# One inverse root for two norms in a row, and a norm's weight and bias applied where its rows are turned

## The chip, the cores and the metric

The kernel runs on one core of a Trainium2 chip. The metric is the time of the whole kernel on the device in microseconds (us), as the median of several runs. The core's engines are TensorE (PE; its weight loads are PEld), VectorE (DVE), ScalarE (ACT), GpSimd (POOL) and SyncE (SP, which here only issues transfers).

## What is computed

Input x has 4 sequences of 1024 rows with 128 columns. Two blocks follow each other:

```python
x = _layernorm(x + mamba(x))            # selective scan, 256 channels x 16 states
x = _layernorm(x + attention_and_moe(x))

# attention_and_moe(hidden_states), cut:
resid = hidden_states
x = layer_norm(hidden_states, ln1_w, ln1_b)
...                                     # causal attention, 16 heads of 8
hidden = resid + (ctx @ o_w + o_b)
resid = hidden
xt = layer_norm(hidden, ln2_w, ln2_b)
logits = xt @ router_w                  # 16 experts, top 2, limited capacity
...
h = gelu(xin @ fc1_w + fc1_b)           # xin: rows of xt, sorted to experts
...
return resid + moe_out
```

Each norm subtracts a row's mean and divides by the root of its variance plus 1e-5. The norm that ends the first block and ln1, which starts the second, act on the same rows one after the other, with nothing between them.

## The kernel before

**Stages.** A test at the start (lines 164 to 207) bounds the attention scores by the norms of the weights; with these inputs it holds and the first branch of line 1307 runs. There the work goes in halves of a sequence, 512 rows in 4 tiles of 128: 8 halves, named (sequence, half).

1. `front` makes the scan's inputs: projections, convolution, step sizes. They go through DRAM.
2. `scans`: for each half 2 groups of channels with 4 state groups, 8 steps in all. A step on DVE is a product `h = u * b` (`begin`, line 444), four scans (line 454), and a product with `c` (`gather`, line 460); ACT makes the decay `da` (line 448), and PE sums the states (line 464). The first sequence is scanned alone.
3. `after_scans` (line 376) follows each half: gate, the scan's own norm (its inverse root is `ssm_rs`), output projection, residual. Then `normalise_in_pieces` with tag `lnx` ends the first block, in place on the rows `r`, and `on_half` hands them to `inputs`.
4. `inputs` (line 574) is attention's start: the norm `ln1` of `x1` into `xh`, four transposes on PE, an ACT step `xnT` that applies ln1's weight and bias while it leaves PSUM (they are per partition after the turn), and the projections to keys, queries and values, the first two split into three bf16 parts that go through DRAM.
5. `stream` runs attention on PE and ACT: scores, exponent, weighted values.
6. `rest_of_half` (line 733): division by the sums, output projection, residual `hid`, the norm `ln2` into `x2`, its weight and bias as two products of 128x512 with rows broadcast to all partitions, the store (to DRAM, or for the last two halves straight into `xrow`), four transposes, a copy `x2T`, and the router's product.
7. `routing` sends rows to their experts' slots in DRAM by indirect transfers from GpSimd. `experts` runs 16 experts: load 512 rows, transpose them, copy to `xeT`, two matmuls with a Gelu between, and scatter back. A last loop adds, norms and stores.

**Norms.** `normalise_in_pieces` (line 146) does `bn_stats` and `bn_aggr` on DVE for each of 4 tiles, adds the constant to the variances (`_ve`, line 137), raises them to -0.5 on GpSimd in one instruction of 128x4 (`_rs`, line 139), and then, after a `yield USE`, subtracts the mean and multiplies, tile by tile, on DVE (line 156).

**Order.** Once the first sequence is scanned, PE and DVE run in the order in which the program writes their instructions (`tc.manual_schedule(engines=pinned)`); ACT, GpSimd and SyncE are ordered by the framework. The order comes from generators: `scan_row` yields between the parts of a scan step, and after each such part `piece()` (line 1319) advances the other streams. `before` holds `after_scans` with `inputs`, `after` holds `rest_of_half`, `aside` the routing, and `attend` is one step of attention:

```python
for at in (USE, None):
    for s in (before, after, aside, loads):
        advance(s, at)
    if at == USE:
        next(attend)
```

A part behind `yield USE` runs ahead of the piece's attention step, a part behind a plain `yield` after it. So `yield USE` and the plain `yield` that follows take one piece together, and a second `yield USE` takes another piece. Between two pieces lie two scans or one product of a scan step on DVE.

Of the kernel before, what the change touches and what calls it, by code (L numbers as in the profile page):

```python
# [10 lines left out]
F32 = mybir.dt.float32  # L11
BF16 = mybir.dt.bfloat16
I32 = mybir.dt.int32
AF = mybir.ActivationFunctionType
# [37 lines left out]
def mamba_then_moe_block_kernel(ctx: ExitStack, tc: tile.TileContext, a: dict, out: bass.AP):  # L52
# [11 lines left out]
    def load_columns(name, vec, n, pool=const):  # L64
        return load(name, [P, n], vec.rearrange("(n p) -> p n", p=P), pool)
# [80 lines left out]
    def normalise_in_pieces(pool, src, dst, n, tag):  # L146

        st = pool.tile([P, n, 6], F32, tag=tag + "_st", name=tag + "_st")
        mv = pool.tile([P, n, 2], F32, tag=tag + "_mv", name=tag + "_mv")
        for i in range(n):  # L150
            nc.vector.bn_stats(st[:, i, :], src[:, i, :])  # L151
            nc.vector.bn_aggr(mv[:, i, :], st[:, i, :])  # L152
        r = inv_std(pool, mv[:, :, 1], n, tag)
        yield USE
        for i in range(n):
            nc.vector.tensor_scalar(  # L156
                dst[:, i, :], src[:, i, :], mv[:, i, 0:1], r[:, i : i + 1], ALU.subtract, ALU.mult
            )
# [7 lines left out]
    ln1_w = load_columns("ln1_w", a["ln1_w"], 1)  # L166
    ln1_b = load_columns("ln1_b", a["ln1_b"], 1)
    head_rows = load("head_rows", [P, HG], a["c_head_rows"])
    with ExitStack() as ph:
# [139 lines left out]
    def scans(ph, x1_pool, on_scans, on_half, spare_bank=lambda: None):  # L309
# [66 lines left out]
        def after_scans(b, hf, y):  # L376
# [55 lines left out]
            for i in range(TPH):  # L432
                nc.vector.scalar_tensor_tensor(
                    r[:, i, :], pa[:, i * P : (i + 1) * P], rs[:, i : i + 1], r[:, i, :], ALU.mult, ALU.add
                )
            yield from normalise_in_pieces(s2, r, r, TPH, "lnx")
            yield from on_half(b, hf, r)

# [85 lines left out]
    def attention_weights(wts):  # L524


        wq = wts.tile([P, P], F32, tag="wq", name="wq")
        wk = wts.tile([P, P], F32, tag="wk", name="wk")
        for w, wp in ((wq, a["q_w_pad"]), (wk, a["k_w_pad"])):
            nc.sync.dma_start(  # L530
                w.rearrange("m (h d) -> m h d", d=HD),
                wp.rearrange("m g (h r) -> m (g h) r", r=P // HG)[:, :, 0:HD],
            )
        qb = wts.tile([P, 1], F32, tag="qb", name="qb")
        kb = wts.tile([P, 1], F32, tag="kb", name="kb")
# [24 lines left out]
        return wq, wk, qb, kb, wv, wo, wr, vb, ob, sel_b, ln2_w, ln2_b, identb, mask_k  # L560

    def attention(ph, weights):

        wq, wk, qb, kb, wv, wo, wr, vb, ob, sel_b, ln2_w, ln2_b, identb, mask_k = weights
        p1 = ph.enter_context(tc.tile_pool(name="fat1", bufs=1, side="right"))
# [5 lines left out]

        def inputs(b, hf, x1, made):

# [157 lines left out]
        def rest_of_half(e, avs, rows):  # L733
# [75 lines left out]
    def attention_with_maxima(ph):  # L809
# [25 lines left out]
        ob = load("ob", [P, D], a["o_b"].unsqueeze(0).partition_broadcast(P), wts)  # L835
        ln2_w = load("ln2_w", [P, D], a["ln2_w"].unsqueeze(0).partition_broadcast(P), wts)
        ln2_b = load("ln2_b", [P, D], a["ln2_b"].unsqueeze(0).partition_broadcast(P), wts)
        sel_a = load("sel_a", [P, NG, H], a["c_sel_a"], wts)
# [13 lines left out]
        for b in range(B):  # L852
# [119 lines left out]
            for qt in range(2):  # L972
# [28 lines left out]
                normalise(p2, hid, x2, 4, "ln2")  # L1001
                nc.gpsimd.tensor_tensor(x2, x2, ln2_w.unsqueeze(1).to_broadcast([P, 4, D]), ALU.mult)
                nc.gpsimd.tensor_tensor(x2, x2, ln2_b.unsqueeze(1).to_broadcast([P, 4, D]), ALU.add)
                rest = x1[:, t0 : t0 + 4, :]
# [4 lines left out]
                x2T = p2.tile([P, 512], F32, tag="x2T", name="x2T")  # L1009
                nc.scalar.copy(x2T, pt)  # L1010
                pl = bank("pl")
# [220 lines left out]
    def experts(ph, weights, behind, sent, all_sent):  # L1232
# [10 lines left out]
        for e in range(E):  # L1243
# [63 lines left out]
    with tc.If(mild > 0) as cmp:  # L1307

        with ExitStack() as late:
            with ExitStack() as ph:  # L1310
# [39 lines left out]

                def on_half(b, hf, x1):

                    yield from attention_inputs(b, hf, x1, made)
                    stacked, vps = made[b]
                    middle.append(Step(b=b, qt=hf, x1=x1, stacked=stacked, vps=vps))
# [50 lines left out]
    with cmp.Else():  # L1406
        scan_done.clear()
        with ExitStack() as ph:
            bank = work_banks(ph)
            drain = lambda pieces: deque(pieces, maxlen=0)  # L1410

            def store_half(b, hf, x1):
                to_tokens(rest_d, b * TPB + hf * TPH, x1)
                yield
# [86 lines left out]
```

## Time and profile before

| | us |
|---|---|
| median of 3 runs | 1365.01 |
| range of the runs | 1358.34 to 1372.29 |
| span of the profiled execution | 1372.2 |
| PE busy | 941.3 (69%) |
| DVE busy | 899.7 (66%) |
| ACT busy | 644.2 (47%) |
| POOL busy | 257.0 (19%) |

The rows of the norms and of what the change touches, from the groups of instructions (line, engine, operation, tiles and shapes, count; then total and mean in ns of one; then the idle time ahead of it and what ended it):

```profile
L156 DVE TENSOR_SCALAR xh<-x,ln_mv,ln_rs 128x128 f32<-128x128 f32 x32 | 8.9, 342 | 5.6 <-POOL ln_rs L139 5.6
L151 DVE BATCH_NORM_STATS2 ln_st<-x 128x6 f32<-128x128 f32 x32 | 8.6, 267 | 0.0
L152 DVE BATCH_NORM_AGGREGATE ln_mv<-ln_st 128x2 f32<-128x6 f32 x64 | 11.6, 182 | 2.1
L783 DVE TENSOR_TENSOR x<-x,ln_w 128x512 f32<-128x512 f32 x8 | 5.5, 692 | 0.3
L1255 DVE COPY xeT<-pt_xe 128x512 f32<-128x512 f32 x16 | 10.3, 682 | 0.0
```

The profile names `x1` and `r` as `x`, and the tags `ln1` and `ln2` both as `ln`: `ln_st<-x` belongs to ln1 and `ln_st<-hid` to ln2. How the profile's other views are read is said where they are shown.

### The profile page before, as it was taken

How to read it: one execution, taken by the hardware profiler on the slowest of the kernel's cores; microseconds unless marked ns; L12 is line 12 of the kernel's file. 1: busy time of each engine (PE TensorE's matmuls, PEld its weight loads, DVE VectorE, ACT ScalarE, POOL GpSimd, SP SyncE). 2: the span in 40 equal slices, each digit the busy share in tenths (PEclk: the TensorE clock that was granted, in tenths of full speed). 3: DMA queues.
4: the chain of work that ended last, by engine and by line, in shares of the span. 5: the costliest groups of instructions: out<-in, count | busy, mean ns of one | idle time of the engine just before them, and what ended most of it. 6: DMA issues, size and time to landing. Idle time of an engine off the chain costs nothing. (4 is left out here: it accounts for less than half of the span.)

```text
span 1372.2 us, 14838 instructions
## 1 busy us (share of the span) xinstructions
PE 941.3 (69%) x5100; PEld 431.3 (31%) x5100; DVE 899.7 (66%) x1407; ACT 644.2 (47%) x887; POOL 257.0 (19%) x232
## 2 busy tenths in 40 slices
PE   4687552477998985688886589688488343699920
PEld 2232210143333333233334224235132012466620
DVE  2299789888977987887998996883461025111136
ACT  1457663246855863466772287652147220133300
POOL 0021011111101012102001110100004712344421
PEclk9898875658987997789896589878579565799965
DMA  3963667363614533443452431320755102222142
GB/s 83 339 213 131 233 215 241 119 188 111 194 60 132 158 104 109 138 133 119 139 160 91 135 114 45 93 60 26 197 159 166 50 18 87 76 66 64 41 115 87
DMA packets 171157, 171.81 MB, mean 125 GB/s; under 512 B 33424, under 2 KB 125840, under 8 KB 170944
## 3 DMA queue, kind: packets, MB, share of 16 engines
q1 hardware_dynamic: 153664, 142.94, 34.9%
q10 hardware_dynamic: 13312, 19.40, 3.9%
q0 software_dynamic: 4096, 8.43, 1.9%
q8 instruction: 42, 0.69, 0.2%
q14 instruction: 43, 0.35, 0.1%
HBM read 111.27 MB, written 59.44 MB: 124 GB/s over the span
## 5 line engine op out<-in xcount | busy, mean ns | idle before, releaser
L690 ACT ACTIVATE pr<-pst 128x1024 f32<-128x1024 f32 (+3 forms) x384 | 293.1, 811 | 130.9 <-PE pst L686 71.1
L680 PE MATMUL pst<-qst,kst 72*128 72x512 bf16 (+3 forms) x768 | 204.1, 366 | 53.4 <-ACT pr L690 39.3
L448 ACT ACTIVATE da<-dt_sp,a_neg 128x512 f32<-128x512 f32 x256 | 178.2, 720 | 122.8 <-DVE h L454 112.4
L697 PE MATMUL av<-pr,vp 128*32 128x512 f32 (+3 forms) x1536 | 188.8, 562 | 7.3 <-issue 4.0
L444 DVE TENSOR_TENSOR h<-u_sp,bt 128x2048 f32<-128x2048 f32 x64 | 145.3, 2274 | 18.4 <-DMA u_sp<-u_d 18.4
L454 DVE TENSOR_TENSOR_SCAN h<-da,carry,h 128x512 f32<-128x512 f32 x128 | 155.9, 1266 | 1.7 <-ACT da L448 1.7
L454 DVE TENSOR_TENSOR_SCAN h<-da,h 128x512 f32<-128x512 f32 x128 | 148.6, 1207 | 6.6 <-ACT da L448 6.6
L460 DVE TENSOR_TENSOR h<-h,ct 128x2048 f32<-128x2048 f32 x64 | 146.2, 2285 | 1.2 <-POOL carry L457 0.3
L464 PE MATMUL py<-h,sel 128*32 128x512 f32 x512 | 90.5, 787 | 72.8 <-DVE h L460 54.7
L680 PEld LDWEIGHTS <-kst 72*128 72x128 bf16 x768 | 65.2, 105 | 205.6 <-issue 186.5
L457 POOL COPY carry<-h 128x4 f32<-128x4 f32 x32 | 43.7, 1365 | 288.5 <-DVE h L454 288.5
L1260 ACT ACTIVATE hT<-ph,b 128x512 f32<-128x512 f32 x64 | 44.0, 687 | 107.3 <-PE ph L1259 105.8
L114 POOL DMA_INDIRECT xin<-xrow,put x64 | 62.1, 971 | 102.8 <-DVE same_e L1138 30.3
L139 POOL TENSOR_TENSOR ln_rs<-ln_ve,neg_half 128x4 f32<-128x4 f32 x16 | 34.6, 2161 | 238.9 <-DVE ln_ve L137 238.9
L114 POOL DMA_INDIRECT eout<-eo,to x64 | 61.4, 960 | 83.2 <-DVE eo L1271 49.1
L686 PE MATMUL pst<-mask_k,identb 128*128 128x128 bf16 x512 | 76.0, 235 | 0.0
L259 PE MATMUL pt_x<-xT,w_tap 128*128 128x512 f32 x128 | 61.6, 639 | 19.1 <-DMA xT<-in_xT_dram 9.8
L1259 PE MATMUL ph<-xeT,w 128*128 128x512 f32 x128 | 61.1, 610 | 8.1 <-DVE xeT L1255 7.5
L1266 PEld LDWEIGHTS po_e<-w,hT 128*128 128x128 f32 x512 | 61.5, 192 | 13.5 <-issue 12.3
L1266 PE MATMUL po_e<-w,hT 128*128 128x128 f32 x512 | 63.2, 276 | 0.1
L686 PEld LDWEIGHTS <-identb 128*128 128x128 bf16 x512 | 51.9, 107 | 32.7 <-issue 11.2
L1103 DVE COPY tot<-ptot 128x64 f32<-128x64 f32 (+1 forms) x6 | 2.0, 333 | 85.7 <-PE ptot L1100 85.7
(218 smaller groups left out, 1126.9 us busy)
## 6 DMA issues: line engine op xcount, KB each, us to landing
dt_sp<-dt_d SPq DMA_DIRECT2D x64, 256.0 KB
u_sp<-u_d SPq DMA_DIRECT2D x64, 256.0 KB
kst<-k_parts SPq DMA_DIRECT2D x96, 144.0 KB
qst<-q_parts SPq DMA_DIRECT2D x64, 144.0 KB
bt<-bc_d SPq DMA_DIRECT2D x32, 256.0 KB
ct<-bc_d SPq DMA_DIRECT2D x32, 256.0 KB
w<-in_fc_w_dram SPq DMA_DIRECT2D x32, 256.0 KB
xin<-clear SPq DMA_DIRECT2D x8, 516.0 KB
```

What stands on the lines that cost most here:

```text
L114: ins = nc.gpsimd.indirect_dma_start(out=dst[:, :], out_offset=bass.IndirectOffsetOnAxis(ap=rows, axis=0), in_=src, in_offset=None).ins
L259: nc.tensor.matmul(pt[:, cols], lhsT=w_tap[:, k, c * P : (c + 1) * P], rhs=xT[:, cols.start + k : cols.stop + k], start=(k == 0), stop=(k ...
L444: nc.vector.tensor_tensor(s.h, s.u, four(s.bt), ALU.mult)
L448: nc.scalar.activation(s.da[jl], s.dt[:, jl, :], AF.Exp, scale=a_neg[:, j, s.g : s.g + 1])
L454: ins = nc.vector.tensor_tensor_scan(h, s.da[jl], h, from_, ALU.mult, ALU.add).ins
L460: nc.vector.tensor_tensor(s.h, s.h, four(s.ct), ALU.mult)
L464: nc.tensor.matmul(s.py[jl * NR : (jl + 1) * NR, :], lhsT=sel, rhs=s.h[:, jl, :], start=(s.g == 0), stop=(s.g == NG_S - 1),)
L680: nc.tensor.matmul(pst[:, jj, :w], lhsT=ks[ki // TPH][jp][:, jj, ki % TPH * P : (ki % TPH + 1) * P], rhs=qs[jp][:, jj, q0:], start=True, s ...
L686: nc.tensor.matmul(pst[:, jj, :P], lhsT=identb, rhs=mask_k, start=False, stop=True)
L690: nc.scalar.activation(pr[:, :, :w], pst[:, :, :w], AF.Exp, scale=QSCALE)
L697: nc.tensor.matmul(av[32 * j : 32 * j + 32, q0:], lhsT=e.vps[ki // TPH][:, ki % TPH, v0 : v0 + 32], rhs=pr[:, jj, :w], start=(ki == 0), st ...
L1266: nc.tensor.matmul(po[:, i, :], lhsT=hT[:, c, i * P : (i + 1) * P], rhs=w2[e][:, c, :], start=(c == 0), stop=(c == NFC - 1),)
```

## The change

It does two things.

The rows that `lnx` would give have mean 0 and variance v/(v+e), where v is the variance of `r` and e = 1e-5. So ln1's factor on `r` itself is 1/sqrt(v + e) times 1/sqrt(v/(v+e) + e), which is 1/sqrt(v(1+e) + e*e). Both factors now come from one set of statistics: two small additions on DVE make `ve[0]` and `ve[1]`, and one power on GpSimd of 128x8 gives both. `inputs` first makes `xh` straight from `r` with the second factor, and later, behind `xnT`, norms `r` in place with the first for the residual.

The weight and bias of ln2 are no longer multiplied into the rows. They are loaded as columns at the start, and applied where the turned rows leave PSUM: in `x2T` for the router (ACT, with scale and bias) and in `xeT` for the experts (DVE, a `tensor_scalar` with two per-partition operands in place of a copy). The stored rows and the expert slots hold the plain norm.

```diff
+        mv = statistics(pool, src, n, tag)
+        r = inv_std(pool, mv[:, :, 1], n, tag)
+        yield USE
+        apply_norm(src, dst, mv, r, n)
...
     ln1_b = load_columns("ln1_b", a["ln1_b"], 1)
+    ln2_w = load_columns("ln2_w", a["ln2_w"], 1)
+    ln2_b = load_columns("ln2_b", a["ln2_b"], 1)
...
-            yield from normalise_in_pieces(s2, r, r, TPH, "lnx")
-            yield from on_half(b, hf, r)
+            mv = statistics(s2, r, TPH, "lnx")
+            ve = s2.tile([P, 2, TPH], F32, tag="lnx_ve", name="lnx_ve")
+            nc.vector.tensor_scalar(ve[:, 0, :], mv[:, :, 1], LN_EPS, None, ALU.add)
+            nc.vector.tensor_scalar(ve[:, 1, :], mv[:, :, 1], 1.0 + LN_EPS, LN_EPS * LN_EPS, ALU.mult, ALU.add)
+            inv = s2.tile([P, 2, TPH], F32, tag="lnx_rs", name="lnx_rs")
+            nc.gpsimd.tensor_tensor(
+                inv.rearrange("p k i -> p (k i)"), ve.rearrange("p k i -> p (k i)"), neg_half[:, : 2 * TPH], ALU.pow
+            )
+            yield USE
+            yield from on_half(b, hf, r, lambda dst, k: apply_norm(r, dst, mv, inv[:, k, :], TPH))
...
-        ln2_w = load("ln2_w", [P, D], a["ln2_w"].unsqueeze(0).partition_broadcast(P), wts)
-        ln2_b = load("ln2_b", [P, D], a["ln2_b"].unsqueeze(0).partition_broadcast(P), wts)
...
             xh = p1.tile([P, 4, D], F32, tag="tok", name="xh")
-            yield from normalise_in_pieces(p1, x1, xh, TPH, "ln1")
+            norm(xh, 1)
             yield
...
             yield USE
             nc.scalar.activation(xnT, pt, AF.Identity, bias=ln1_b, scale=ln1_w)
+            norm(x1, 0)
             yield
...
-            yield from normalise_in_pieces(p1, hid, x2, 4, "ln2")
-            nc.vector.tensor_tensor(x2, x2, ln2_w.unsqueeze(1).to_broadcast([P, 4, D]), ALU.mult)
             to = x2 if rows.xrow is None else rows.xrow[:, t0 : t0 + 4, 0:D]
-            nc.vector.tensor_tensor(to, x2, ln2_b.unsqueeze(1).to_broadcast([P, 4, D]), ALU.add)
+            yield from normalise_in_pieces(p1, hid, to, 4, "ln2")
...
-            nc.scalar.copy(x2T, pt)
+            nc.scalar.activation(x2T, pt, AF.Identity, bias=ln2_b, scale=ln2_w)
...
-            nc.vector.tensor_copy(xeT, pt)
+            nc.vector.tensor_scalar(xeT, pt, ln2_w, ln2_b, ALU.mult, ALU.add)
```

The branch that runs when the scores are not bounded has the same edits for ln2 and a `norm(x1, 0)` ahead of its store; it doesn't run here.

More of the change, by code (lines that the diff above doesn't have):

```diff
@@ L146, in normalise_in_pieces, with statistics @@
     def normalise_in_pieces(pool, src, dst, n, tag):
+        mv = statistics(pool, src, n, tag)
+        r = inv_std(pool, mv[:, :, 1], n, tag)
+        yield USE
+        apply_norm(src, dst, mv, r, n)
+    def statistics(pool, src, n, tag):
         st = pool.tile([P, n, 6], F32, tag=tag + "_st", name=tag + "_st")
@@ L152, in normalise_in_pieces, with apply_norm @@
             nc.vector.bn_aggr(mv[:, i, :], st[:, i, :])
-        r = inv_std(pool, mv[:, :, 1], n, tag)
-        yield USE
+        return mv
+    def apply_norm(src, dst, mv, r, n):
         for i in range(n):
@@ L559, in attention_weights @@
         )
-        return wq, wk, qb, kb, wv, wo, wr, vb, ob, sel_b, ln2_w, ln2_b, identb, mask_k
+        return wq, wk, qb, kb, wv, wo, wr, vb, ob, sel_b, identb, mask_k
     def attention(ph, weights):
-        wq, wk, qb, kb, wv, wo, wr, vb, ob, sel_b, ln2_w, ln2_b, identb, mask_k = weights
+        wq, wk, qb, kb, wv, wo, wr, vb, ob, sel_b, identb, mask_k = weights
         p1 = ph.enter_context(tc.tile_pool(name="fat1", bufs=1, side="right"))
@@ L572, in attention, with inputs @@
         ps_av = ph.enter_context(tc.tile_pool(name="fps_av", bufs=1, space=PSUM, side="right"))
-        def inputs(b, hf, x1, made):
+        def inputs(b, hf, x1, norm, made):
             if hf == 0:
@@ L835, in attention_with_maxima @@
         ob = load("ob", [P, D], a["o_b"].unsqueeze(0).partition_broadcast(P), wts)
-        ln2_w = load("ln2_w", [P, D], a["ln2_w"].unsqueeze(0).partition_broadcast(P), wts)
-        ln2_b = load("ln2_b", [P, D], a["ln2_b"].unsqueeze(0).partition_broadcast(P), wts)
         sel_a = load("sel_a", [P, NG, H], a["c_sel_a"], wts)
@@ L1001, in attention_with_maxima @@
                 normalise(p2, hid, x2, 4, "ln2")
-                nc.gpsimd.tensor_tensor(x2, x2, ln2_w.unsqueeze(1).to_broadcast([P, 4, D]), ALU.mult)
-                nc.gpsimd.tensor_tensor(x2, x2, ln2_b.unsqueeze(1).to_broadcast([P, 4, D]), ALU.add)
                 rest = x1[:, t0 : t0 + 4, :]
@@ L1009, in attention_with_maxima @@
                 x2T = p2.tile([P, 512], F32, tag="x2T", name="x2T")
-                nc.scalar.copy(x2T, pt)
+                nc.scalar.activation(x2T, pt, AF.Identity, bias=ln2_b, scale=ln2_w)
                 pl = bank("pl")
@@ L1349, in mamba_then_moe_block_kernel, with on_half @@
                 rows = Step(xrow=None, stored=0)
-                def on_half(b, hf, x1):
-                    yield from attention_inputs(b, hf, x1, made)
+                def on_half(b, hf, x1, norm):
+                    yield from attention_inputs(b, hf, x1, norm, made)
                     stacked, vps = made[b]
@@ L1410, in mamba_then_moe_block_kernel, with store_half @@
             drain = lambda pieces: deque(pieces, maxlen=0)
-            def store_half(b, hf, x1):
+            def store_half(b, hf, x1, norm):
+                norm(x1, 0)
                 to_tokens(rest_d, b * TPB + hf * TPH, x1)
```

## The prediction

> **What bounds the kernel now.** I read the page's slices first, then the busy times by stage, then who VectorE (DVE) waited for in the longest stage, then instructions in order of time around one norm. Slices (two of the rows) and stages:
>
> ```profile
> PE   4687552477998985688886589688488343699920
> DVE  2299789888977987887998996883461025111136
> ```
>
> ```profile
> core 0: us, PE busy (x) PEld busy (x) DVE busy (x) ACT busy (x) POOL busy (x), PEclk, DMA share, GB/s
> 268.00:930.00 662.00, 520.39 (x3256) 220.89 (x3256) 565.40 (x702) 397.83 (x577) 88.39 (x53) 0.82 0.39 118
> 930.00:1005.00 75.00, 46.44 (x229) 24.39 (x228) 35.97 (x106) 19.59 (x29) 5.62 (x8) 0.71 0.52 134
> 1005.00:1120.00 115.00, 78.46 (x444) 27.09 (x444) 17.78 (x63) 49.77 (x66) 46.31 (x48) 0.70 0.32 95
> 1192.00:1320.00 128.00, 112.79 (x651) 81.80 (x649) 22.04 (x52) 39.89 (x59) 61.44 (x64) 0.99 0.19 56
> ```
>
> From 268 to 930 us the scans of batches 1 to 3 run beside attention. DVE is busy 565.4 of 662 us (85%), more than TensorE (PE), and each piece of the interleaving carries some 2.3 us of scan work on it. From 930 to 1192 nothing is full: one chain of small steps. From 1192 to 1320 the experts fill PE. What DVE waits for in the first of these (three of the rows):
>
> ```profile
> DVE x L397 <- PE pb L388: 20.6, 5, 8.1
> ...
> DVE x L156 <- POOL lnx_rs L139: 4.5, 5, 0.9
> DVE xh L156 <- POOL ln_rs L139: 4.5, 5, 0.9
> ```
>
> All rows of that answer together come to 82 us, 61 of them on PE. One norm pair on DVE, and its two powers on GpSimd (POOL):
>
> ```profile
> 268.91 1.09 DVE L156 TENSOR_SCALAR x<-x,lnx_mv,lnx_rs 128x128 f32<-128x128 f32 x4
> 269.91 0.29 DVE L151 BATCH_NORM_STATS2 ln_st<-x 128x6 f32<-128x128 f32 x1
> ...
> 271.71 2.28 DVE L444 TENSOR_TENSOR h<-u_sp,bt 128x2048 f32<-128x2048 f32 x1
> 274.90 1.12 DVE L156 TENSOR_SCALAR xh<-x,ln_mv,ln_rs 128x128 f32<-128x128 f32 x4 [0.90 <-POOL ln_rs L139]
> ```
>
> ```profile
> 266.83 1.85 POOL L139 TENSOR_TENSOR lnx_rs<-lnx_ve,neg_half 128x4 f32<-128x4 f32 x1 [3.96 <-DVE lnx_ve L137]
> ...
> 271.89 2.98 POOL L139 TENSOR_TENSOR ln_rs<-ln_ve,neg_half 128x4 f32<-128x4 f32 x1 [2.61 <-DVE ln_ve L137]
> ```
>
> The statistics of the second norm hold DVE from 269.91 to 271.71 less their overlap, 1.8 us. A power beside scans takes 1.85 us and is done before DVE wants it; beside the product with two inputs it takes 2.98 us and DVE waits 0.90 us; later, with DVE idle, the same power takes 1.01 us. In the chain after the scans the pair stands on the path by itself:
>
> ```profile
> 962.30 1.12 DVE L156 TENSOR_SCALAR x<-x,lnx_mv,lnx_rs 128x128 f32<-128x128 f32 x4 [1.12 <-POOL lnx_rs L139]
> ...
> 965.11 0.17 DVE L137 TENSOR_SCALAR ln_ve<-ln_mv 128x4 f32<-128x4 f32 x1
> 966.41 0.86 DVE L156 TENSOR_SCALAR xh<-x,ln_mv,ln_rs 128x128 f32<-128x128 f32 x3 [1.13 <-POOL ln_rs L139]
> ```
>
> [...] the trace has 584 ns for the copy x2T (L794) and 778 for the same size with both (xnT, L593), 97 each.
>
> **The change part by part.** There are 8 halves of rows. Stepping through the generators by hand (a piece is one call that advances every stream), the scans end at piece 196 in both kernels. In the first 196 lie the lnx/ln1 pairs of 7 halves and the ln2 of 5; after them come the pair of the last half and three ln2.
>
> 1. Second statistics and second power go. Per half 4 bn_stats (0.267) and 4 bn_aggr (0.182) at 0.449 = 1.80 us; 7 halves: 12.6 us of DVE. The second small tensor_scalar on the variance takes the place of the one removed, and no more.
> 2. Waits for the power. Before, 5 + 5 of the 14 in this stage had a product before their use: 10 x 0.90 = 9.0 us. After, by the order of instructions, 5 of the 7 combined powers stand behind a product and 2 behind two scans. The combined power has 8 columns, not 4, and no trace row shows that size. Floor: it costs as 4 do, wait 0.90. Ceiling: twice, 2.0 us after the product lets it go, wait 1.9 (and 1.1 in the two behind scans). I take 1.5 and 0.2, since a part of 1.01 us must be per instruction (a 128x4 copy on POOL shows 0.22): 5 x 1.5 + 2 x 0.2 = 7.9. Gain 1.1 us; at the ends 4.5 gained or 2.7 lost. Behind the waiting apply stand all later scans on DVE, so this wait is real time there.
> 3. The two ln2 products of 0.69 us leave DVE: 1.38 per half, 5 halves, 6.9 us.
> 4. Sum in the scan stage: 12.6 + 1.1 + 6.9 = 20.6 us of DVE time. DVE is the last to finish in most pieces but not all; where the next thing is one of the waits on PE, the time saved is waited out there. With 85% busy I credit 80%: 16 us.
> 5. After the scans, on the chain. Pair of the last half: from 962.30, when the first apply starts, to 966.41, when xh starts, is 4.1 us; the combined power may be 0.6 longer and the second addition is 0.1: 3.4 us gained. The apply to x1 now follows behind xnT, where DVE had 2.57 us idle before `rest`. The three ln2: 1.4 each, as the transposes wait for them, less 0.2 once for x2T with both operands on the last: 4.0. Together 7.4 us.
> 6. Order. The pair needs a piece less, so xh, keys and queries come one piece earlier and the pieces drop from 259 to 258. That is the same time as in 4 and 5 seen from the planner, so I add nothing; but for the whole stage PE work and DVE work face each other differently.
> 7. Costs. Two column loads stand ahead of wq at the start; SyncE issues one per 0.47 us there, the mild test waits for wq and wk, so 0.9 us. The two broadcast loads that go (1.25 and 0.44 us of issue near 36 us) lie before a wait on the front's u at 46 us, so they return nothing. In the experts xeT becomes a tensor_scalar from PSUM: 746 ns by the row of L294 against 682, 0.064 x 16 = 1.0 us at most; PE is full there and the transposes run an expert ahead, so I take 0.3. x2T on the other halves: 0.2 us of ACT, behind its 71 us of waits for PE. The branch without the mild bound doesn't run.
>
> Forecast: 1365.0 - 16 - 7.4 + 0.9 + 0.3 = 1342.8, say **1343 us**.
>
> **The rivals.**
> - *PE gains as well* (0.22): PE stood idle 54.0 us in 7 waits for xh (7.7 each) in the scan stage. xh comes earlier by the first apply 1.1, statistics 1.8, wait 0.9 and one scan step 2.3 = 6.1 us on DVE, while PE has one attention step of 3.8 us less ahead of it: 2.3 us less idle, 16 in all. If most of that shortens DVE's own waits on PE: 1365 - 20.6 - 7.4 + 1.2 - 11 = 1327. Against it: in some of these halves attention has nothing to do, and PE's idle time is free.
> - *Handed to the next wait* (0.20): 61 us of DVE's 82 are waits on PE, and 8.1 us is the longest. If these take two thirds of the scan gain: 1365 - 6.9 - 7.4 + 1.2 = 1352.
> - *Slower* (0.08): the power costs twice (7 us over my value), and the new order meets a stall. In the last half's attention ACT stood 3.72, 8.13, 10.64 and 7.48 us with no engine named as holder:
>
> ```profile
> 1073.92 0.59 ACT L725 COPY avs<-av 128x512 f32<-128x512 f32 x1 [8.13 <-remote]
> ...
> 1091.43 1.02 ACT L690 ACTIVATE pr<-pst 128x1024 f32<-128x1024 f32 x1 [10.64 <-issue]
> ```
>
>   Another 30 us of that kind gives 1343 + 7 + 30 = 1380. Against it: nothing in the change touches that stretch; it could as well shrink.
>
> **How the numbers follow.** Likeliest case 0.50 at 1343, with 0.22, 0.20 and 0.08 for the others. Faster by over 1% means below 1351.4: nearly all of the first (0.45), all of the second (0.22), a quarter of the third (0.05): 0.72. Within 1%: 0.05 + 0.15 + 0.01 = 0.21. Slower: 0.07. The range takes in 1327 and 1352 with the measurement's spread (1358.3 to 1372.3 before) on either side: 1320 to 1363.
>
> **What would show it.** In the changed profile: bn_stats `ln_st<-x` gone, DVE's busy time down by about 25 us (8 x 1.8 + 8 x 1.38 = 25.4); lnx_rs as 128x8, between 1.0 and 2.0 us with DVE idle, and DVE's waits on it near 8 us; the stretch from lnx_ve to xh of the last half 3.4 us shorter; the last scan some 15 us earlier than before; xeT near 746 ns. It would be wrong if the last scan came no earlier, if DVE's waits on PE in the scan stage grew beyond 61 us by what was saved, or if the attention of the last half took much more or less than its 115 us.

## The result, and the profile after

| kernel | median us | range | ratio to before, 95% interval |
|---|---|---|---|
| before, in the first measurement | 1363.18 | 1358.34 to 1372.29 | |
| changed, first measurement | 1326.15 | 1320.17 to 1332.51 | 0.9721 [0.9651, 0.9791] |
| changed, second measurement | 1319.01 | 1308.61 to 1327.22 | 0.967 [0.9605, 0.9736] |
| changed, third measurement | 1301.48 | 1290.05 to 1309.72 | 0.9674 [0.9643, 0.9706] |

The change makes the kernel 37, 45 and 41 us faster. The forecast said 22 us (1343) in a range that ends at 1320; the rival "PE gains as well" said 1327. Chips differ by up to 26 us in the same kernel (before: 1342 to 1368), so below a kernel is compared with the kernel before on its own chip, by ratio; differences in us are between medians, unless they are said to be by the ratio. The profiled execution of the kernel before is its slowest and that of the changed kernel its fastest, so the two spans (1372.2 and 1318.2) lie 54 us apart where the medians lie 37.

The page of the changed kernel, the busy tenths of TensorE and VectorE in 40 slices:

```profile
PE   5687751468899895698886599787497542889920
DVE  2299799898978987896989897893370034212146
```

The busy times by stage of the changed kernel, in windows set by hand where the stages of the kernel before were (scans beside attention, end of the scans, attention of the last half, experts):

```profile
core 0: us, PE busy (x) PEld busy (x) DVE busy (x) ACT busy (x) POOL busy (x), PEclk, DMA share, GB/s
268.00:888.00 620.00, 511.43 (x3244) 215.23 (x3244) 542.87 (x630) 395.45 (x575) 73.79 (x44) 0.83 0.42 126
888.00:950.00 62.00, 41.03 (x208) 21.72 (x205) 25.38 (x72) 12.83 (x22) 4.00 (x6) 0.71 0.39 93
950.00:1065.00 115.00, 81.20 (x475) 27.42 (x474) 24.94 (x82) 56.81 (x74) 47.56 (x49) 0.75 0.45 132
1138.00:1266.00 128.00, 112.08 (x649) 81.44 (x647) 23.69 (x52) 39.37 (x58) 60.76 (x64) 0.98 0.18 56
```

The first of them is 620 us long instead of 662, with VectorE as full as it was (542.87 of 620 is 88%, 85% before). Part of these 42 us is the hand-set cut; the cut by events below gives 22 to 30. The last two windows have their old length by choice. From the last `lg` (the router's product leaves PSUM) to the end of the kernel, which takes in the experts, the traces have 219.1 us against 218.7. VectorE's waits in the first of these stages (us in all, times, longest):

```profile
DVE hid L794 <- PE pt_po L789: 15.4, 4, 5.0
DVE x L406 <- PE pb L397: 11.2, 2, 6.0
...
DVE xh L163 <- POOL lnx_rs L452: 6.5, 5, 1.5
```

The wait on `pb` was 20.6 us; it is 21.5 again in the run below that only puts the piece back, so it went with the order. The waits for the power, 4.5 + 4.5 before, are now 6.5. The larger move is on the other engine. TensorE's waits in the kernel before (268 to 930 us), and then in the changed one (268 to 888 us):

```profile
PE pt_xn L590 <- DVE xh L156: 54.0, 7, 11.2
```

```profile
PE pt_xn L607 <- DVE xh L163: 20.7, 6, 6.0
```

(A seventh wait lies just ahead of 268 us; with it the sum is 24.9.) What makes them is seen in one half of the scan stage. VectorE in the kernel before, from the variance of the first norm to `xh` (start, duration, in brackets the idle time ahead of it and its releaser):

```profile
856.67 0.17 DVE L137 TENSOR_SCALAR lnx_ve<-lnx_mv 128x4 f32<-128x4 f32 x1
856.75 2.28 DVE L444 TENSOR_TENSOR h<-u_sp,bt 128x2048 f32<-128x2048 f32 x1
859.94 1.11 DVE L156 TENSOR_SCALAR x<-x,lnx_mv,lnx_rs 128x128 f32<-128x128 f32 x4 [0.90 <-POOL lnx_rs L139]
...
862.69 0.17 DVE L137 TENSOR_SCALAR ln_ve<-ln_mv 128x4 f32<-128x4 f32 x1
862.76 2.29 DVE L460 TENSOR_TENSOR h<-h,ct 128x2048 f32<-128x2048 f32 x1
865.95 1.12 DVE L156 TENSOR_SCALAR xh<-x,ln_mv,ln_rs 128x128 f32<-128x128 f32 x4 [0.90 <-POOL ln_rs L139]
```

And the same half in the changed kernel:

```profile
827.80 0.17 DVE L449 TENSOR_SCALAR lnx_ve<-lnx_mv 128x4 f32<-128x4 f32 x1
...
827.95 2.29 DVE L463 TENSOR_TENSOR h<-u_sp,bt 128x2048 f32<-128x2048 f32 x1
831.77 1.12 DVE L163 TENSOR_SCALAR xh<-x,lnx_mv,lnx_rs 128x128 f32<-128x128 f32 x4 [1.53 <-POOL lnx_rs L452]
```

From `lnx_ve` to `xh` are 9.28 us before and 3.97 us after; in the seven halves of the stage it was 8.32 to 9.28 and is 2.83 to 3.97. Of the 5.3 us between, 1.8 are statistics and 1.1 the first norm's own step. The other 2.4 come with the second power: the order puts a scan product of 2.28 us between a power and its use, and VectorE waits behind it. TensorE, in order, stood 7.48 us at the transposes of this `xh` before and 3.72 after, with scan and attention matmuls queued behind them.

For a fair cut the stage is measured below from the third to the last `y` (a finished output of the scans), by each kernel's own trace. The last three rows belong to experiments of the next section:

| kernel | us | DVE busy | DVE waits | of these on PE, on POOL | PE's waits on DVE | of these for `xh` | `lnx_ve` to `xh` in one half | clock |
|---|---|---|---|---|---|---|---|---|
| before | 701.0 | 599.6 | 95.6 | 75.8, 10.4 | 126.5 | 54.0 | 9.28 | 0.81 |
| changed, first trace | 670.9 | 585.2 | 80.5 | 62.2, 9.2 | 90.9 | 24.9 | 3.97 | 0.82 |
| changed, third trace | 678.9 | 585.1 | 89.0 | 68.3, 9.2 | 92.7 | 24.9 | 3.97 | 0.81 |
| norm part alone | 695.5 | 591.9 | 98.6 | 77.4, 9.2 | 97.8 | 25.1 | 3.96 | 0.79 |
| changed, piece put back | 670.1 | 581.0 | 79.2 | 74.5, 1.4 | 98.8 | 26.3 | 4.56 | 0.82 |
| changed, second power put back | 690.0 | 582.8 | 97.2 | 76.1, 14.2 | 108.1 | 40.1 | 7.23 | 0.81 |

(The clock is TensorE's mean granted clock in the stage, as a share of full speed.) Even this cut does not hold quite the same work. In the changed kernel `xh` comes a piece earlier, and so the residual and the ln2 statistics of one more half (24 `ln_st<-hid` instead of 20, some 3.5 us of VectorE in all) lie ahead of the last `y`. The two kernels with a piece put back have the instructions of the kernel before there, but for what the change removes or the experiment adds.

### The profile page after: what moved, and what is told of

Same layout as the page of the kernel before. It is cut to its first block, busy times and chain, and to the rows that moved or that the text cites. A ratio compares the mean times of both kernels' runs of the same rounds, so it can differ in the third digit from the quotient of the medians.

```text
span 1318.2 us, 14741 instructions
## 1 busy us (share of the span) xinstructions
PE 932.8 (71%) x5100; PEld 424.6 (32%) x5100; DVE 878.5 (67%) x1327; ACT 644.7 (49%) x887; POOL 245.4 (19%) x224
## 4 chain that ended last, share of the span: by engine, by line
PE 32%; DVE 17%; issue 12%; POOL 8%; ACT 6%; DMA 6%; SPq 2%; another core or an unknown queue 1%; DVEq 0%; ACTq 0%; POOLq 0%
PE av L715 9%; PE pst L698 8%; DVE h L473 5%; POOL eout L114 4%; ACT pr L708 4%; PE po L782 2%; PE py L483 2%; PE pt_yc L415 2%; DVE h L479 2%; SPq L636 2%; POOL lnx_rs L452 2%; PE pst L704 2%; PE pa L397 1%; DMA qst<-q_parts 1%
## 5 line engine op out<-in xcount | busy, mean ns | idle before, releaser
L715 PE MATMUL av<-pr,vp 128*32 128x512 f32 (+3 forms) x1536 | 193.6, 575 | 4.4 <-issue 3.5
L473 DVE TENSOR_TENSOR_SCAN h<-da,carry,h 128x512 f32<-128x512 f32 x128 | 155.9, 1268 | 1.7 <-ACT da L467 1.7
L483 PE MATMUL py<-h,sel 128*32 128x512 f32 x512 | 85.2, 744 | 75.3 <-DVE h L479 53.3
L715 PEld LDWEIGHTS av<-pr,vp 128*32 128x32 f32 x1536 | 35.8, 115 | 62.4 <-issue 42.5
L139 POOL TENSOR_TENSOR ln_rs<-ln_ve,neg_half 128x4 f32<-128x4 f32 x8 | 17.9, 2240 | 204.1 <-DVE ln_ve L137 169.3
```

The costliest lines, as they stand in the source:

```text
L473: ins = nc.vector.tensor_tensor_scan(h, s.da[jl], h, from_, ALU.mult, ALU.add).ins
L483: nc.tensor.matmul(s.py[jl * NR : (jl + 1) * NR, :], lhsT=sel, rhs=s.h[:, jl, :], start=(s.g == 0), stop=(s.g == NG_S - 1),)
L715: nc.tensor.matmul(av[32 * j : 32 * j + 32, q0:], lhsT=e.vps[ki // TPH][:, ki % TPH, v0 : v0 + 32], rhs=pr[:, jj, :w], start=(ki == 0), st ...
```

## The experiments

Three chips were used: the first four kernels below and the last ran on one, the next four on a second, the three after those on a third. All ratios are to the kernel before, timed beside them.

**The two parts alone.** The kernel before with only the norm's edits, and with only ln2's:

```diff
-            yield from normalise_in_pieces(s2, r, r, TPH, "lnx")
-            yield from on_half(b, hf, r)
+            mv = statistics(s2, r, TPH, "lnx")
...
+            yield from on_half(b, hf, r, lambda dst, k: apply_norm(r, dst, mv, inv[:, k, :], TPH))
```

> The kernel before with the norm part alone (one set of statistics, one power of 8 columns, xh straight from r); ln2 as before. Theory 'work' (only the DVE time removed counts, credited at 80%, order neutral): 0.8 x 13.7 + 3.4 = 14 us off, ratio 0.990. Theory 'order' (a piece less between the statistics and xh also takes PE's idle time away): 25 to 30 us off, ratio 0.979. PE's wait for xh in the scan stage falls from 54 us to about 21 either way.

Measured: 1324.54 us, 0.9841 [0.9805, 0.9877], 21.4 us by the ratio, between the two theories. TensorE's wait for `xh` fell to 25.1 us, about as expected, but VectorE's waits on TensorE did not fall with it (77.4 us, 75.8 before; this trace has the lowest clock of the table).

```diff
-            nc.vector.tensor_tensor(x2, x2, ln2_w.unsqueeze(1).to_broadcast([P, 4, D]), ALU.mult)
-            nc.vector.tensor_tensor(to, x2, ln2_b.unsqueeze(1).to_broadcast([P, 4, D]), ALU.add)
...
+            nc.scalar.activation(x2T, pt, AF.Identity, bias=ln2_b, scale=ln2_w)
...
+            nc.vector.tensor_scalar(xeT, pt, ln2_w, ln2_b, ALU.mult, ALU.add)
```

> The changed kernel with the norm part put back as it was (lnx in place, then ln1 with its own statistics and power); ln2's weight and bias applied at the turn. Theory 'work': 0.8 x 6.9 + 4.0 - 1.2 = 8 us off, ratio 0.994. Theory 'order': the same 8 us, since no piece is saved here. If the loads moved at the start matter by themselves, the first scan starts 2 us earlier here and not in the run with the norm part alone.

Measured: 1329.08 us, 0.9892 [0.9866, 0.9918], 14.5 us by the ratio. The product of the two ratios is 0.9735. That lies within the first and second intervals of the whole change, and 0.003 above the third, which was measured on the same chip: the parts add up or fall a little short. Each is 6 to 7 us larger than the forecast's steps.

**The piece put back** in the changed kernel, so that there are 259 pieces again:

```diff
             yield USE
+            yield USE
             yield from on_half(b, hf, r, lambda dst, k: apply_norm(r, dst, mv, inv[:, k, :], TPH))
```

> The changed kernel with a second USE step behind the power: all removed instructions stay removed, but xh is again made a piece later and the pieces number 259 as before. Theory 'work': as the changed kernel or a little faster (DVE never waits for the power), ratio to before 0.972. Theory 'order': 10 to 15 us of the gain go back, ratio 0.980 to 0.983.

Measured: 1307.38 us, 0.9725 [0.9685, 0.9766], as "work" had it. On the same chip the changed kernel has 1301.48 (0.9674): the piece is worth some 6 us, within intervals that overlap. Here two products lie between the variance and `xh`, the power is done before it is wanted, and the stretch is 4.56 us (VectorE, and then the two waits of the stage that bear on the argument):

```profile
829.23 0.17 DVE L449 TENSOR_SCALAR lnx_ve<-lnx_mv 128x4 f32<-128x4 f32 x1
...
829.38 2.29 DVE L464 TENSOR_TENSOR h<-u_sp,bt 128x2048 f32<-128x2048 f32 x1
831.58 2.29 DVE L480 TENSOR_TENSOR h<-h,ct 128x2048 f32<-128x2048 f32 x1
833.79 1.10 DVE L163 TENSOR_SCALAR xh<-x,lnx_mv,lnx_rs 128x128 f32<-128x128 f32 x4
```

```profile
DVE x L406 <- PE pb L397: 21.5, 5, 7.1
```

```profile
PE pt_xn L608 <- DVE xh L163: 26.3, 7, 7.5
```

VectorE's wait on `pb` is back where it was (20.6 us before), although TensorE stands for `xh` hardly longer than in the changed kernel. The other traces agree: in the five kernels with as many pieces as before, VectorE waits 20.6 to 24.9 us on `pb` and 6.8 to 8.5 us on TensorE ahead of `hid`, while TensorE stands for `xh` anything from 19 to 55 us. In those with fewer pieces it is 8.7 to 16.2 and 13.6 to 20.1 us, and in the one with more 9.2 and 12.0. So these two waits follow the order of the pieces, and not how long TensorE stood at the transposes.

**The second statistics put back**, read by nobody:

```diff
+            statistics(p1, x1, TPH, "ln1")
             norm(xh, 1)
```

> The changed kernel with the four bn_stats and bn_aggr of ln1 put back ahead of xh, their result unused: the new order with the old DVE work. Theory 'work': 12.6 us in the scan stage and 1.8 after it come back, less what the wait for the power hides (1.3 us in five halves): about 8 us slower than the changed kernel, ratio 0.978. Theory 'order': as little as 4 us slower, ratio 0.975.

Measured: 1309.84 us, 0.9742 [0.9717, 0.9767], 8 us over the changed kernel on the same chip, with 0.001 between the intervals. The 8 us are those of "work", the ratio is nearer to that of "order", since the changed kernel itself came out lower than both had it. The statistics fill the time in which VectorE waited for the power, and `xh` is no later (838.55 to 842.52 us, 3.97 as without them):

```profile
838.63 0.16 DVE L450 TENSOR_SCALAR lnx_ve<-lnx_mv 128x4 f32<-128x4 f32 x1
838.70 2.28 DVE L463 TENSOR_TENSOR h<-u_sp,bt 128x2048 f32<-128x2048 f32 x1
840.90 0.28 DVE L157 BATCH_NORM_STATS2 ln_st<-x 128x6 f32<-128x128 f32 x1
...
842.52 1.11 DVE L163 TENSOR_SCALAR xh<-x,lnx_mv,lnx_rs 128x128 f32<-128x128 f32 x4
```

So 14.4 us of work (8 x 1.80) cost about 8, since the 8.6 us of waiting for the power, over the whole run, went.

**The changed kernel again, on the second chip:**

> The changed kernel once more, without any edit, as the base of the three kernels timed with it on this chip. Its ratio to the kernel before was 0.972 in its first measurement and every theory expects 0.970 to 0.975 here. The added piece and the unused statistics gave 0.9725 and 0.9742 in their own measurement, so their cost against the changed kernel is known only as well as this ratio.

Measured: 1319.01 us, 0.967 [0.9605, 0.9736], a little under what was expected.

**The second power put back**, without statistics:

```diff
+            ve2 = s2.tile([P, TPH], F32, tag="ln1_ve", name="ln1_ve")
+            nc.vector.scalar_tensor_tensor(ve2, inv[:, 1, :], 0.0, ve[:, 1, :], ALU.mult, ALU.add)
+            inv2 = s2.tile([P, TPH], F32, tag="ln1_rs", name="ln1_rs")
+            nc.gpsimd.tensor_tensor(inv2, ve2, neg_half[:, :TPH], ALU.pow)
+            yield USE
```

> The changed kernel with the second power of the kernel before put back in series, and no statistics: xh waits for a 128x4 power whose operand needs the result of the 128x8 one, with a piece boundary behind it as before (258 pieces become 259, as in the added piece). Theory 'DVE work': the gain of the norm part is the 1.80 us of statistics per half that VectorE no longer does, so a second power costs only its wait on VectorE, some 0.9 us in each of the 7 halves of the scan stage and 1.9 us in the last: 8 us, ratio 0.978. Theory 'chain': the gain is that xh, and so TensorE's transposes and all the attention behind them, come earlier by the length of the removed chain, and the unused statistics, which cost little, did not bring that chain back; then a second power in series brings back most of the norm part's 21 us: ratio 0.984 to 0.988, and TensorE's wait for xh (25 us in the scan stage) returns towards 54 us.

Measured: 1347.88 us, 0.9881 [0.9852, 0.9911]: 29 us over the changed kernel on its chip, and 0.0156 (21 us) over the kernel with the same piece put back and no power, on the first chip. That is as much as the whole norm part gave (ln2 alone: 0.9892), with next to no VectorE work. The piece's runs had 0.015 more clock than the kernel before beside them and these 0.006, which by the slope given with the last experiment would be some 8 of the 21 us. VectorE in one half:

```profile
849.56 0.17 DVE L449 TENSOR_SCALAR lnx_ve<-lnx_mv 128x4 f32<-128x4 f32 x1
...
849.71 2.29 DVE L470 TENSOR_TENSOR h<-u_sp,bt 128x2048 f32<-128x2048 f32 x1
853.52 0.16 DVE L457 SCALAR_TENSOR_TENSOR ln_ve<-lnx_rs,lnx_ve 128x4 f32<-128x4 f32 x1 [1.53 <-POOL lnx_rs L452]
853.60 2.28 DVE L486 TENSOR_TENSOR h<-h,ct 128x2048 f32<-128x2048 f32 x1
856.79 1.11 DVE L163 TENSOR_SCALAR xh<-x,lnx_mv,ln_rs 128x128 f32<-128x128 f32 x4 [0.90 <-POOL ln_rs L459]
```

The stretch is 7.23 us, 3.26 more than in the changed kernel: 2.28 of product, 0.90 of wait, the rest the operand. Over the stage (690.0 us) the kernel to compare it with is the one with the piece put back (670.1), which has the same instructions there but for the power and its operand. VectorE's busy time is 582.8 against 581.0. Its waits are 97.2 against 79.2: 12.8 more on POOL (14.2 against 1.4), 3.6 more on ACT and 1.6 more on PE. VectorE's and then TensorE's waits in that stage:

```profile
DVE x L406 <- PE pb L397: 24.9, 5, 8.4
...
DVE ln_ve L457 <- POOL lnx_rs L452: 8.3, 7, 1.5
DVE xh L163 <- POOL ln_rs L459: 4.5, 5, 0.9
```

```profile
PE pt_xn L614 <- DVE xh L163: 40.1, 7, 9.2
```

TensorE stands 14 us more at the transposes than with the piece alone (40.1 against 26.3), but VectorE hardly waits longer on TensorE for it (76.1 against 74.5). In these two traces the larger part of what the power costs in the stage, 12.8 of 19.9 us, is VectorE's own wait for GpSimd. "DVE work" (8 us) fell by its size: it counted one wait of 0.9 us a half where two fall due in most halves, 1.53 and 0.90 in the one shown. "Chain" came within 0.001 of its range, yet its sign, a wait for `xh` near 54 us, did not come. The run asks for somewhat more than the kernel before had: its two powers are of 128x8 and 128x4 in series, and VectorE waits 14.2 us on POOL where it waited 10.4 us for two of 128x4.

**ln2's two products put back**, behind the turned rows and read by nobody:

```diff
             nc.scalar.activation(x2T, pt, AF.Identity, bias=ln2_b, scale=ln2_w)
+            dead = p1.tile([P, 4, D], F32, tag="dead", name="dead")
+            nc.vector.tensor_tensor(dead, to, vb.unsqueeze(1).to_broadcast([P, 4, D]), ALU.mult)
+            nc.vector.tensor_tensor(dead, dead, vb.unsqueeze(1).to_broadcast([P, 4, D]), ALU.add)
```

> The changed kernel with two VectorE products of 128x512 put back per half behind the turned rows of the second norm, into a tile that nobody reads (any 128-column operands will do, the result is unused): they cost VectorE 1.38 us per half, and nothing waits for them. Theory 'DVE work': in the scan stage VectorE's time is the stage's, so the 5 halves there cost 6.9 us and the 3 behind the scans little: ratio 0.977. Theory 'chain': what the removal of the products gave (14.5 us when made alone) is mostly that the second norm's rows reach TensorE earlier; off that path the products cost 3 us or less: ratio 0.972 to 0.974.

Measured: 1333.67 us, 0.9807 [0.9747, 0.9867], 14.7 us over the changed kernel on that chip, with 0.001 between the intervals; the two traces differ by 7.5 us (1327.0 and 1319.5), 5.2 of it in the scan stage (676.2 and 671.0) with 6.6 more VectorE busy. "Chain" (3 us or less) is not borne out: off the path, too, this work, 11.0 us in all (8 x 1.38), is paid for.

**The power cut in two, `xh`'s factor first:**

```diff
+            nc.vector.tensor_scalar(ve[:, 1, :], mv[:, :, 1], 1.0 + LN_EPS, LN_EPS * LN_EPS, ALU.mult, ALU.add)
+            nc.gpsimd.tensor_tensor(inv[:, 1, :], ve[:, 1, :], neg_half[:, :TPH], ALU.pow)
+            nc.vector.tensor_scalar(ve[:, 0, :], mv[:, :, 1], LN_EPS, None, ALU.add)
+            nc.gpsimd.tensor_tensor(inv[:, 0, :], ve[:, 0, :], neg_half[:, :TPH], ALU.pow)
```

> The changed kernel with its 128x8 power cut in two of 128x4, xh's factor first, so that xh waits for half the power: 1.01 us instead of 1.64 us with VectorE idle[...]. Theory 'DVE work' (a wait of VectorE counts as its work does): 0.6 to 1.2 us less wait in each of 8 halves, 5 to 9 us: ratio 0.965 to 0.968. Theory 'chain': the same 0.6 to 1.2 us per half off the chain to xh, and the same ratio. Theory 'hidden': the wait of 1.5 us per half is filled by other engines' work, and nothing changes: ratio 0.972.

Measured: 1318.8 us, 0.9688 [0.9619, 0.9757], no gain in the medians; without its slowest run the median is 1314.55, 4.5 us less than the changed kernel's 1319.01, at a clock of 0.804 against 0.8005. The wait fell from 6.8 to 3.6 us and the stage from 671.0 to 667.2 in the traces; an effect of that size lies below what these runs resolve. The 1.2 us a half at the upper end was the author's estimate. The traces have the two sizes of power 0.63 us apart, with VectorE idle (1.01 and 1.64) and beside a product (2.98 and 3.61), and in the half shown above `xh` waited 1.53 us in the changed kernel and 0.90 here.

**The transposes a piece later**, in the kernel before and in the changed one, so that TensorE has other matmuls to do ahead of them:

```diff
+            yield USE
             yield
             pt = bank("pt_xn")
```

> The kernel before, unchanged in all it computes, with one more piece between the making of xh and its transposes, so that TensorE has the scan's and an attention step's matmuls (about 4 us) to do ahead of the transposes instead of standing idle for xh. Theory 'queue behind the transposes': the norm part gains because TensorE, in order, stands for xh with scan and attention work queued behind it (54 us in 7 halves of the scan stage), and VectorE afterwards waits for that work; then this kernel, which takes no work from any engine, gains up to 25 us of it: ratio 0.982 to 0.990, TensorE's wait for xh under 30 us. Theory 'chain': what counts is how soon xnT, keys and queries are there, and these now come a piece (5 us) later: ratio 1.01 to 1.03. Theory 'DVE work': nothing changes on VectorE: ratio 1.00.

> The changed kernel with the same added piece between xh and its transposes. The wait of TensorE for xh was 25 us in the scan stage and should fall below 8 us. Theory 'queue behind the transposes': half or more of that is won, 10 to 20 us, ratio 0.955 to 0.963 where the changed kernel has 0.970. Theory 'chain': slower by the later keys and queries, ratio 0.98 or more. Theory 'DVE work': ratio 0.970.

Measured: 1353.95 us, 0.9881 [0.9845, 0.9916] in the kernel before; 1332.54 us, 0.9715 [0.968, 0.975] in the changed one. The first ratio is as "queue behind the transposes" had it, but TensorE's wait for `xh` fell only from 54.0 to 38.7, not under 30. These runs had a clock 0.013 above that of the kernel before, which by the slope given below is 11 of the 14 us between the medians. In the changed kernel the wait fell from 25 to 19, not under 8, and nothing was won. So order alone is not shown to give more than a small part of the gain.

**No piece between power and `xh`:**

```diff
-            yield USE
             yield from on_half(b, hf, r, lambda dst, k: apply_norm(r, dst, mv, inv[:, k, :], TPH))
```

> The changed kernel without the piece boundary between the 128x8 power and xh: no scan product lies between them on VectorE, so the power runs with VectorE idle (1.64 us instead of 3.0) and the stretch from lnx_ve to xh falls from 4.0 to 2.0 us in each of 7 halves, while VectorE waits 1.8 instead of 1.5 us; TensorE comes to the transposes one attention step (about 3.8 us) earlier as well. Theory 'DVE work': 2 us slower, ratio 0.972. Theory 'chain': 2 us or more earlier per half, 14 us, ratio 0.958 to 0.962. Theory 'queue behind the transposes': TensorE arrives 3.8 us earlier and xh only 2.0 us, with the product behind it, so its wait for xh grows by up to 2 us per half from 25 to 35 or 40 us: ratio 0.975 to 0.985.

Measured: 1335.04 us, 0.9753 [0.9718, 0.9787]. The stretch fell to 1.99 us as meant,

```profile
834.98 0.17 DVE L449 TENSOR_SCALAR lnx_ve<-lnx_mv 128x4 f32<-128x4 f32 x1
835.06 0.16 DVE L450 TENSOR_SCALAR lnx_ve<-lnx_mv 128x4 f32<-128x4 f32 x1
836.97 1.12 DVE L163 TENSOR_SCALAR xh<-x,lnx_mv,lnx_rs 128x128 f32<-128x128 f32 x4 [1.75 <-POOL lnx_rs L452]
```

and the kernel is not 14 us faster than the changed one (0.967 to 0.972) but level with it or slower, so "chain" falls as a rule. The ratio is at the lower edge of what "queue behind the transposes" had, but its sign did not come: TensorE's wait for `xh` stayed at 24.7 us. VectorE's waits on POOL in the stage rose from 9.2 to 14.4. "DVE work" (0.972) lies within the interval too. How soon `xh` is there does not decide by itself; which of the waits does, these runs don't tell.

**The changed kernel a third time, and the granted clock:**

> The changed kernel a third time, without an edit, to part the granted clock from the rest. In the three jobs of experiments so far, runs of one and the same kernel spread with the TensorE clock that the throttle granted them: pooled over 116 runs, -867 us for a clock of 1.0 more (standard error 96), that is 8.7 us for 0.01; and the kernels differ in the clock they get, before 0.791 to 0.799, the changed kernel and its variants 0.796 to 0.814. Theory 'work and chain': the changed kernel is 36 to 38 us faster at the same clock too, as in its second measurement (44.6 us, of which 0.009 of clock gives 7.8). Theory 'clock': what goes beyond the forecast's 22 us is the granted clock; at the same clock it is 20 to 26 us faster, as its variants with the piece put back, with the unused statistics and with the transposes a piece later were (22.7, 26.3 and 22.0 us when corrected in this way). The ratio itself is expected at 0.967 to 0.975 by both.

Measured: 1301.48 us against 1342.32, 0.9674 [0.9643, 0.9706]. The median granted clocks are 0.8075 and 0.800; at 867 us per 1.0 that is 6.5 of the 40.8 us, and 34.3 are left. "Clock" (20 to 26 left) fell; "work and chain" (36 to 38) is near. About 7 us of the gain, here and in the second measurement, went with a clock that the changed kernel was granted and the kernel before was not. Time and clock go together in runs of the same kernel; no run sets the clock, so that the one makes the other is not shown, and why these kernels are granted more stays open. The correction also leaves the parts short of the whole: at the same clock the norm part alone gives 16 us and ln2 alone 4, the change 34 to 37.

No kernel tried is shown to be faster than the changed one.

## Why the prediction was right, and where its sizes were off

Direction, range and most of the steps held. The size (22 us forecast, 37 to 45 measured) went to the rival that it had put second, 1327 us forecast and 1326 measured. That is in part luck: some 7 us went with the clock, which no step had in it, and the rival's way, from less idle time of TensorE to shorter waits of VectorE, is not shown (step 4). Of the signs, `ln_st<-x` is gone, VectorE's busy time fell by 21.2 us (25 forecast), and the last `y` comes 34 us earlier in the traces (15 forecast).

1. *Second statistics* (12.6 us in the scan stage, 80% of it credited, and 1.8 in the last half, 12 in all). Put back alone they cost 8 us. With the second power there as well they cost nothing that shows: both together are the kernel with ln2 alone, 0.9892, and the power alone is at 0.9881 (ln2 alone had the higher clock, for which the slope gives some 5 us).
2. *Waits for the power.* The size was right: 7.9 us forecast in the stage, 6.8 measured, the wait 1.53 beside a product where 1.5 was taken. The 128x8 power lies within the bounds for VectorE idle (1.64, between 1.0 and 2.0). GpSimd in the changed kernel beside a product, and then with VectorE idle:

```profile
828.12 3.61 POOL L452 TENSOR_TENSOR lnx_rs<-lnx_ve,neg_half 128x8 f32<-128x8 f32 x1 [6.04 <-DVE lnx_ve L450]
```

```profile
919.18 1.64 POOL L452 TENSOR_TENSOR lnx_rs<-lnx_ve,neg_half 128x8 f32<-128x8 f32 x1 [5.28 <-DVE lnx_ve L450]
```

   What the second power gave is the term that was mis-sized. The step credited its loss with 1.1 us in the scan stage, as the difference of two waits, and step 6 put the product that the order lays beside it at nothing. As the difference of waits it was right (10.4 us on POOL before, 9.2 after). But put back, a second power cost 21 to 29 us in all and 19 in the stage, some 8 of which may be the clock: VectorE waits once more in most halves, and `xh` comes 1.3 to 4.3 us later than in the changed kernel, 23 us in the 8 halves together. How these two share in the cost is not parted.
3. *ln2's products* (6.9 us in the stage). Their work is paid for off the path too, by 7.5 us in the trace. The part alone gave 14.5 us; its runs had a clock of 0.810 against 0.799, for which 10 us is the estimate by the slope above, so how it divides stays open.
4. *The credit of 80%.* For the change as a whole this step was wrong. It let VectorE's waits on PE take back a fifth of what VectorE saves, but the stage fell by 22 to 30 us while VectorE's busy time fell by 14.5 (19.5 in steps 1 and 3; with the piece put back, where the work compares, by 18.6, and the stage by 30.9). All waits of VectorE together fell from 95.6 to 80.5 and 89.0 us in the changed kernel and to 79.2 with the piece put back. Which of them fell differs: in the changed kernel those on PE (75.8 to 62.2 and 68.3), with the piece put back those on POOL and ACT (PE 74.5). With the norm part alone the sum did not fall (98.6). TensorE's waits on VectorE fell from 126.5 to between 90 and 99 in all these traces, so they do not by themselves shorten VectorE's. Why the waits fell stays open. For VectorE work alone the share held in the one run that adds nothing else: ln2's products put back took 6.6 us of VectorE and 5.2 of the stage.
5. *After the scans.* The pair came out exactly. VectorE in the changed kernel's last half:

```profile
918.86 0.17 DVE L449 TENSOR_SCALAR lnx_ve<-lnx_mv 128x4 f32<-128x4 f32 x1
...
920.85 1.12 DVE L163 TENSOR_SCALAR xh<-x,lnx_mv,lnx_rs 128x128 f32<-128x128 f32 x4 [1.75 <-POOL lnx_rs L452]
```

   From `lnx_ve` to `xh` are 1.99 us where there were 5.41, 3.4 less. What the three ln2 gave can't be told from the stalls in that stretch (next section).
6. *Order, "I add nothing".* Between the last `y` of the scans and the last `ssm_ve` (the variance of the scan's own norm, which opens the last half's chain) lie 22.4 us before and 15.2 after; with the piece put back it is 21.3 again. That is no gain on top of step 4, since the work has moved ahead of the last `y`. From the third `y` to the last `ssm_ve` the traces have 723.4 us before, 686 to 695 in the changed kernel and 691.4 with the piece put back. By the medians the piece is worth 6 us (1307.38 against 1301.48), which the intervals do not part from nothing. It does order VectorE's waits anew, as the step had warned.
7. *Costs.* The first product of the scans starts at 61.66 us, 63.57 before; over all traces it starts between 60.4 and 63.7, so the 0.9 us forecast can't be seen. `x2T` took 773 ns with weight and bias and 584 as a copy, 0.19 us more where the forecast took 0.2. `xeT` is dearer than the row taken for it, 803 ns and not 746, but the part from the last `lg` to the end is as long as it was:

```profile
L1268 DVE TENSOR_SCALAR xeT<-pt_xe,ln_w,ln_b 128x512 f32<-128x512 f32 x16 | 12.3, 803 | 0.0
```

The mean gain of three measurements is 41 us. An estimate of its parts: the forecast's 22, some 7 with the clock, and 12 that the runs don't divide between the second power, the order and VectorE's shorter waits. The rival "PE gains as well" had expected 16 us less idle time of PE at `xh`; it was 29.

## What to carry to other kernels

Where engines work through hand-written orders that wait on each other, a removed step can be worth more than its own busy time: one small power (2.99 us of GpSimd in the half shown), with its wait and what the order laid beside it, cost 21 to 29 us when it came back. Read the waits of both engines, and compare them only between kernels that have the same order: moving a piece changed which waits VectorE has more than TensorE's idle time did (its wait on `pb` was 20.6 us before and 21.5 with the piece put back, with TensorE idle for `xh` 54.0 and 26.3 us, but 11.2 in the changed kernel at 24.9). A shorter stretch is no gain by itself: 7.23 to 3.97 us went with 29 us, 3.97 to 1.99 with none. Work put into a wait of the same engine cost less than its size here: 14.4 us of statistics, where VectorE had waited 8.6 us for one power, cost some 8.

## What the runs showed of the hardware

- The power of GpSimd took 1.01 us for 128x4 and 1.64 for 128x8 with VectorE idle, so doubling the columns added 0.63. Under scans the two took 1.85 and 2.48 us. Where VectorE had begun a scan product of 128x2048 (two inputs) just ahead of the power, they took 2.98 and 3.61 us, with 0.87 and 1.49 of it behind the product's end, and `xh` started 0.90 and 1.53 us behind that end. Not every power beside a product took longer: one of 128x8 in the changed kernel that began 0.42 us ahead of the product (at 722.25 us) took 1.64, and `xh` did not wait for it.
- In runs of one kernel the time goes with the granted TensorE clock: 122 runs of 15 groups give 8.7 us less for 0.01 more (standard error 0.9; in the changed kernel's third measurement 1290.05 us at 0.824 and 1308.83 at 0.804), and the clock's median differs between kernels on one chip by up to 0.016 (0.791 in the kernel before, 0.8065 in the changed one with the transposes later).
- The stalls of ACT without a named holder in the last half's attention, which the rival "Slower" had quoted, went with the chip. They are in all seven traces of experiments from the second and third chip, and in none of the five from the first (that of the first two traces isn't on record; both have them). ACT's waits in that stretch, in the changed kernel on the second chip,

```profile
ACT pr L708 <- PE av L715: 13.4, 5, 4.7
...
ACT pr L708 <- remote: 9.9, 4, 4.9
...
ACT avs L743 <- remote: 5.3, 1, 5.3
```

  and on the first, where no `remote` is among them:

```profile
ACT pr L708 <- PE pst L704: 8.8, 11, 4.1
ACT pr L708 <- PE pst L698: 7.7, 9, 2.3
ACT avs L743 <- PE av L715: 2.1, 4, 0.5
```

  The stretch from the last `vp` to the last `lg` is 155.9 us on the one and 137.8 us on the other, about the 17.5 us between this kernel's medians there; on the first chip alone the stretch varies from 129.3 to 146.0 between kernels. What makes the stalls wasn't tried.
